# Strassen's seven half products for eight in the attention scores of the first two chunks

## The chip, the cores and the metric

The kernel runs on one core of a Trainium2 chip. The metric is the device time of one execution in microseconds. A core has five engines with a queue each: TensorE (PE, with its weight loads shown as PEld), VectorE (DVE), ScalarE (ACT), GpSimd (POOL) and SyncE (SP), and 16 DMA engines that move data between HBM and the on-chip memory. [...]

## The reference

A graph of N = 2708 nodes with 512 features goes through four layers, each followed by a residual and a layer norm. Layer 2 is two attention layers in a row, and the change is in these alone:

```
proj = x @ W                      # W: 512 x 1024
Wh, Ws = jnp.split(proj, 2, axis=-1)
scores = Wh @ Ws.T                # 2708 x 2708, contraction over 512
a = softmax(scores, axis=-1) * adj
out = a @ Wh + x
x = leaky_relu(out, 0.01)
```

adj is a sparse 0/1 matrix of about 16 neighbours a node, so a has few entries that count. Everything is float32.

## The kernel before

Nodes are cut in 22 blocks of 128 rows (the last has 20), and the columns of a product in six chunks `CH` of 512, 512, 512, 512, 384 and 276 nodes. Both weight halves of an attention layer are multiplied into one 512x512 matrix (`mix`), so that scores are x M x^T. `project_steps` (L1491) computes for each chunk k four tiles `wst[k][c]`, c being the quarter of the contraction, of 128 x 512, and the rows `z` = Wh, which go to a table `pairs` in HBM.

`layer` (L1827) then walks over the six chunks. For chunk k, `load_moving` (L1542) brings the four tiles `xs` (128 x chunk) that stream through PE. `scores` (L1552) computes the scores of one block of 128 nodes against the whole chunk: four matmuls (c = 0..3) of weights 128x128 into one PSUM bank, which ACT copies to a page `s`. The order of blocks is 0, 1, 2, 21, 3 to 20. Block 21 with its 20 rows takes one pass of four small matmuls side by side (`few`, L673) and four adds by DVE. `greatest` (L1578) keeps a running maximum `top` over the blocks. In the next chunk's walk `shift_rows` (L1586) transposes `top` after block 1, reduces and broadcasts it (`wide`), and `shift_columns` transposes `wide` back after block 2 and copies it to `shift`.

From block 3 on, `soften` (L1623) works on the chunk before, one or two steps after each block: DVE subtracts `shift`, ACT takes Exp, DVE adds to the sum and multiplies by the mask (one byte a node, `load_masks` brings all six groups at once), and SP stores the block to `pairs`. When a chunk is softened, `fetch` (L1677) lets POOL gather by an index list the few rows of `pairs` that a block of nodes needs, with at most ten gathers ahead, and `weigh` (L1732) multiplies them on PE into `acc`, between the score products of later chunks. `end` (L1768) divides, adds the residual and stores. After the last chunk the rest is softened and weighed between the work of a filler: the projection of the second attention layer, or the first products of layer 3.

The order of the instructions on every engine is written out: class `Ordered` (L54) chains each engine's instructions in the order in which the program issues them. Where in the walk a gather is weighed is decided by a clock that counts the ideal time of products (`advance`, with `cost(columns)` = 4 x columns / 2400 us) and takes a gather to need 1.15 us and to land 6 us later. No measured time enters. Tiles of on-chip memory come from a pool of 82 pages of 2 KB a partition, PSUM from two halves of four banks (`bank`): score products take half 0, and `acc`, transposes and the like take half 1. A page or bank that is used again makes the first writer wait for its last readers.

All engine work is recorded at one helper line, L71, in the profile; groups are told apart by their tiles: sp for score products, acc for the sparse products of the outer layers and for the weighing (acc<-g), z and wst for projection, mm for the dense products.

Of the kernel before, what the change touches and what calls it, by code (L numbers as in the profile page):

```python
# [19 lines left out]
P = 128  # L20
# [22 lines left out]
PAGES, WIDES = 82, 11  # L43
# [44 lines left out]
class Kernel:  # L88


    def __init__(self, ctx, tc, x_in, x_t, adj, adj_t, w0, b0, w1, b1, w2, w2_t, w3, b3, out):
        self.tc, self.nc = tc, tc.nc
        nc = self.nc
        self.ctx = ctx
        self.x_in, self.x_t, self.adj, self.adj_t, self.out = x_in, x_t, adj, adj_t, out
        self.w0, self.b0, self.w1, self.b1, self.w2 = w0, b0, w1, b1, w2
        self.w2_t, self.w3, self.b3 = w2_t, w3, b3
        const = ctx.enter_context(tc.tile_pool(name="const", bufs=1))
        self.small = ctx.enter_context(tc.tile_pool(name="small", bufs=4))
        scratch = ctx.enter_context(tc.tile_pool(name="scratch", bufs=1, space=DRAM))  # L100
        tile_ = lambda name, shape, dt: const.tile(shape, dt, tag=name, name=name)
        self.ident = tile_("ident", [P, P], FP)
        self.ones = tile_("ones", [P, P], FP)
        self.ones_b = tile_("ones_b", [P, P], BF)

        self.rdeg = tile_("rdeg", [P, NB], FP)
        self.dis = tile_("dis", [P, NB], FP)
        self.nbad = len(CH) * NB
        self.bad = tile_("bad", [P, self.nbad + NB], FP)


        self.feeds = tile_("feeds", [P, NB, QUARTERS, NB], BF)
        self.givers = tile_("givers", [P, NB, LISTS], I32)

        self.base = tile_("base", [P, QUARTERS], FP)
        self.upto = tile_("upto", [P, P], BF)
        self.node = tile_("node", [P, 1], FP)
        self.block = tile_("block", [P, NB], BF)
        self.since = tile_("since", [P, P], BF)
        self.saved = [  # L120
            [scratch.tile([P, D], FP, tag=f"x{s}_{i}", name=f"x{s}_{i}") for i in range(NB)]
            for s in range(3)
        ]
        self.between = [
            scratch.tile([P, D], FP, tag=f"y_{i}", name=f"y_{i}") for i in range(NB)
        ]

        self.masks = [
            scratch.tile([P, NB, w], U8, tag=f"mask{k}", name=f"mask{k}")
            for k, (_, w) in enumerate(CH)  # L130
        ]

        self.turned = [
            [
                scratch.tile([P, DC, w], FP, tag=f"t{s}_{k}", name=f"t{s}_{k}")
                for k, (_, w) in enumerate(CH)
            ]
            for s in range(2)
        ]

    def constants(self, page):
# [4 lines left out]
        nc.gpsimd.memset(self.feeds, 0.0)  # L146
# [313 lines left out]
    def other_weights(self):  # L460


        nc = self.nc
        with self.tc.tile_pool(name="ps_bad", bufs=1, space=PSUM) as ps_bad:
            total = self.small.tile([P, 1], FP, tag="bad_sum", name="bad_sum")
            nc.vector.tensor_reduce(total, self.bad, AX.X, ALU.add)
            ps = ps_bad.tile([P, 1], FP, tag="bad", name="bad_ps")
            nc.tensor.matmul(ps, self.ones, total, start=True, stop=True)
            flag = self.small.tile([P, 1], I32, tag="flag", name="flag")
            nc.vector.tensor_scalar_min(flag, ps, 1.0)  # L470
        return nc.values_load(flag[0:1, 0:1])


def blocks_of(k):

    c0, cw = CH[k]
    return [(c0 // P + q, q * P, min(P, cw - q * P)) for q in range(-(-cw // P))]

# [37 lines left out]
class Fast:  # L516
# [4 lines left out]
    def __init__(self, kernel):  # L521
        self.k, self.tc = kernel, kernel.tc
        self.nc = Ordered(kernel.tc)
        self.notes = []
# [10 lines left out]
    def run(self):  # L535
        kernel, nc = self.k, self.nc
        with ExitStack() as ctx:
# [4 lines left out]
            self.small, self.lists = pool("small_f", 4), pool("lists", 1)  # L542
# [295 lines left out]
    def note(self, k, g, at):  # L838

        (c0, cw), (j0, j1) = CH[k], GROUPS[g]  # L840
        feeds = self.k.feeds.rearrange("p i q j -> p j (i q)")
        i0, full = c0 // QW, cw // QW
        sets = [(j0, j1, P)] if j1 < NB else [(j0, j1 - 1, P), (j1 - 1, j1, QW)]
        for q0, q1, n in ((0, full, QW), (full, -(-cw // QW), cw % QW)):
            for a, b, rows in sets if q0 < q1 else ():
                v = at[:rows, a - j0 : b - j0, q0 * QW : q0 * QW + (q1 - q0) * n]
                self.nc.vector.tensor_reduce(
                    feeds[:rows, a:b, i0 + q0 : i0 + q1],
# [351 lines left out]
    def index(self, k):  # L1200
# [8 lines left out]
        tile_ = lambda tag, shape, dt: self.lists.tile(shape, dt, tag=tag, name=f"{tag}{k}")  # L1209
# [31 lines left out]
        f = kernel.feeds[:, i0 : i0 + n, :, :]  # L1241
        nc.vector.tensor_scalar(f, f, 0.0, None, ALU.not_equal)
        some, a, b = (tile_(t, one, BF) for t in ("some", "a", "b"))
# [13 lines left out]
        kept = tile_("kept", one, BF)  # L1257
# [26 lines left out]
        def examine():  # L1284

            top = tile_("top", [P, n], FP)
# [13 lines left out]
        row, which = tile_("row", one, BF), tile_("which", one, BF)  # L1300
# [5 lines left out]
        sums = tile_("sums", [P, n, 2 * LISTS], FP)  # L1306
# [16 lines left out]
        t = tile_("list", [P, n, LISTS], FP)  # L1323
# [5 lines left out]
    def one_hot(self, s, row, which):  # L1329
# [12 lines left out]
        tile_ = lambda tag, w: self.lists.tile([P, NB, w], BF, tag=tag, name=f"{tag}{s}", bufs=2)  # L1342
        hit, both = tile_("hit", LISTS), tile_("both", 2 * LISTS)
# [13 lines left out]
class Chunk:  # L1357


    def __init__(self, ly, k):  # L1360
# [3 lines left out]
        self.s, self.masks, self.ends = {}, {}, []  # L1364
        self.softened = 0
        self.fetched, self.rden = [], None
# [12 lines left out]
class AttentionLayer:  # L1379
    def __init__(self, number, pairs):  # L1380
        self.number, self.pairs = number, pairs
        self.w, self.mixed, self.xt, self.wst = [], [], {}, {}


class Attention:
# [7 lines left out]
    def __init__(self, fast):  # L1393
# [16 lines left out]
        self.mixed = self.scratch.tile([DC, P, D], FP, tag="mixed", name="mixed")  # L1410
        self.layers = [AttentionLayer(a, self.pairs[a]) for a in range(2)]
        self.clock, self.fetch_free, self.pending = 0.0, 0.0, []

# [77 lines left out]
    def project_steps(self, ly, k):  # L1491
# [4 lines left out]
        for m in range(DC):  # L1496
# [13 lines left out]
            yield True  # L1510
        for i, lo, n in blocks_of(k):
# [29 lines left out]

    def load_moving(self, ch):  # L1542
# [9 lines left out]
    def scores(self, ch, j):  # L1552
# [6 lines left out]
        if n <= QW:  # L1559
            ps = self.f.few(  # L1560
                0, name, n, cw, lambda c: wst[c][:, lo : lo + n], lambda c: ch.xt[c][:, :cw]
            )
            self.f.total(s[:n, :cw], ps, n, cw)
            self.advance(cost(cw))
# [10 lines left out]
        nc.scalar.copy(s[:n, :cw], ps[:n, :cw])  # L1575
        self.advance(DC * cost(cw))

    def greatest(self, ch, j):  # L1578
        n, cw, s = rows_of(j), ch.cw, ch.s[j]
        if j == 1:  # L1580
            ch.top = self.page(f"top{ch.name}")
            self.nc.vector.tensor_max(ch.top[:, :cw], ch.s[0][:, :cw], s[:, :cw])
        elif j > 1:
            self.nc.vector.tensor_max(ch.top[:n, :cw], ch.top[:n, :cw], s[:n, :cw])
# [31 lines left out]
    def load_masks(self, ch):  # L1616
        for j0, j1 in GROUPS:
            a = self.page(f"a{ch.name}_{j0}", U8, (P, DC, ch.cw))
            self.nc.sync.dma_start(a[:, : j1 - j0, :], self.k.masks[ch.k][:, j0:j1, :])
            for j in range(j0, j1):  # L1620
                ch.masks[j] = a[:, j - j0, :]

    def soften(self, ch):  # L1623
# [4 lines left out]
        if v < NB:  # L1628
            if v == 0 and ch.k >= 2:

                assert not self.chunks[ch.k - 2].to_fetch
            n = rows_of(v)
            s = ch.s[v][:n, :cw]
            nc.vector.tensor_sub(s, s, ch.shift[:n, :cw])
            nc.scalar.activation(s, s, AF.Exp)
        j = v - 1
        if j < 0:
            return
        n = rows_of(j)
# [37 lines left out]
    def fetch(self, ch):  # L1677
# [19 lines left out]
        begin = max(self.fetch_free, self.clock + (16 if (q, t) == ch.first_fetch else 0))  # L1697
# [3 lines left out]
    def load_rows(self, ch, q):  # L1701
# [7 lines left out]
        if ch.ly.number == 1:  # L1709
            ch.first[q] = self.page(f"x1{ch.name}_{q}")  # L1710
            self.nc.sync.dma_start(ch.first[q][:w], self.k.saved[1][i][:w])

    def fetch_ahead(self):
        count = sum(len(c.fetched) for c in self.chunks)
        for c in self.chunks:
            while c.to_fetch:
                if c.softened <= NB or count >= self.AHEAD:
                    return
# [13 lines left out]
    def weigh(self, wait=False):  # L1732
# [16 lines left out]
        if first:  # L1749
            ch.acc = self.bank(1, f"acc{ch.name}_{q}")  # L1750
        for h, g in enumerate(gs):
# [74 lines left out]

    def layer(self, ly, chunks, fill):  # L1827
        f = self.f
        self.chunks, self.made = chunks, {}
        for k, ch in enumerate(chunks):  # L1830
            old = chunks[k - 1] if k else None


            js = [0, 1, 2, NB - 1, *range(3, NB - 1)]
            for n, j in enumerate(js):
                if old and n == 0:
                    self.load_masks(old)
                if old and n >= 3:
                    if n == 3 and k >= 3:
                        while chunks[k - 3].to_weigh:  # L1840
                            self.weigh(True)
                    for _ in range(1 + n % 2):
                        if old.softened <= NB:
                            self.soften(old)
                self.scores(ch, j)
# [3 lines left out]
                if n == 4 and k + 1 < len(chunks):  # L1849
                    self.load_moving(chunks[k + 1])  # L1850
                if k + 1 == len(chunks) and n in ((5, 11, 19) if ly.number == 0 else (5, 11)):
                    next(fill)
                if old and n == 0:
                    self.greatest(old, js[-1])
                if n:
                    self.greatest(ch, js[n - 1])
# [4 lines left out]
                if old and n == 1:  # L1861
                    self.shift_rows(old)
                if old and n == 2:
                    self.shift_columns(old)
        last = chunks[-1]
        self.load_masks(last)
        self.greatest(last, js[-1])
# [7 lines left out]

        done = self.clock + (2 if ly.number == 0 else 4)
        while last.softened <= NB:
# [108 lines left out]
```

## Time and profile before

| what | value |
|---|---|
| device time, median of 3 runs | 2330.78 us (2322.93 to 2333.93) |
| span of the profiled execution, first to last instruction | 2297.7 us |
| PE busy | 2269.4 us, 99% of the span |
| DVE, ACT, POOL busy | 1391.5, 675.5, 705.4 us |
| TensorE clock granted, mean | 0.997 |
| score products sp, records of 512, 384 and 276 columns | 1344, 336 and 336 |
| score products sp, busy (a record's overlap with the next counted once) | 589.9, 114.9 and 83.4 us |
| gathers | 510 |

No device time is given for the profiled execution itself; its span is 33.1 us below the median of the runs. Busy time is the union of an engine's records. A float32 matmul leaves two records. A record's own length holds the run through the array, so the pace of back-to-back matmuls is read from the distance of their starts, or from the length of a stretch over its count. In the chain of work that ended last, each piece is what released the next. The lines that the prediction rests on are shown there.

### The profile page before, as it was taken

To read this page: it belongs to the slowest core of one execution; us is meant where nothing else is said; L and a number is where in the kernel's file an instruction comes from. 1 tells how busy PE (TensorE), PEld (TensorE's weight loads), DVE (VectorE), ACT (ScalarE), POOL (GpSimd) and SP (SyncE) were. 2 spreads that over 40 slices of the span, in tenths; PEclk is the share of its full clock that TensorE was granted. 3 is DMA by queue.
4 is the path that set the end of the run, shared out by engine and by line. 5 is a ranking of instruction groups with operands and counts; after the bars stand their busy time and mean duration, and the time that the engine had idled before them with its cause. 6 is when DMAs were issued, how large, how long until landed. Compare 5 with 4: busy or idle time off the path is not lost.

```text
span 2297.7 us, 25903 instructions
## 1 busy us (share of the span) xinstructions
PE 2269.4 (99%) x8525; PEld 1289.0 (56%) x8525; DVE 1391.5 (61%) x2803; ACT 675.5 (29%) x1354; POOL 705.4 (31%) x822
## 2 busy tenths in 40 slices
PE   9999999999999999999999999999999999899997
PEld 6776876777644444443555444444443555466685
DVE  6777787786553537748667511238769788525523
ACT  7444452322111123223322200113223334342211
POOL 3433431111000001635557540001635467442000
PEclk9999999999999999999999999999999999999999
DMA  9966752223547415858789997405868799963311
GB/s 351 286 188 184 199 168 81 76 81 104 208 184 267 144 25 184 303 191 297 254 311 360 349 412 284 183 8 179 303 218 286 254 322 339 334 217 120 116 51 43
DMA packets 260929, 486.34 MB, mean 212 GB/s; under 512 B 40238, under 2 KB 126950, under 8 KB 260784
## 3 DMA queue, kind: packets, MB, share of 16 engines
q1 hardware_dynamic: 192128, 269.63, 33.6%
q0 software_dynamic: 68656, 214.96, 28.0%
q8 instruction: 69, 1.13, 0.2%
q14 instruction: 76, 0.62, 0.1%
HBM read 307.55 MB, written 176.92 MB: 211 GB/s over the span
## 4 chain that ended last, share of the span: by engine, by line
PE 86%; DMA 6%; DVE 4%; ACT 1%; issue 1%; POOL 1%; SPq 0%; ACTq 0%; POOLq 0%; DVEq 0%
PE sp L71 33%; PE acc L71 30%; PE mm L71 8%; PE z L71 6%; PE wst L71 6%; DMA x<-x 2%; DMA x<-in_x 1%; DMA at<-in_adj_t 1%; DMA g<-pairs,givers 1%; PE mix L71 1%; DMA pairs<-s 1%; POOL xt L71 1%; PE list L71 1%; ACT m L71 1%; PE tr_x2t L71 0%
## 5 line engine op out<-in xcount | busy, mean ns | idle before, releaser
L71 PE MATMUL sp<-xs,wst_sb 128*128 128x512 f32 (+3 forms) x2112 | 798.3, 544 | 0.0
L71 POOL DMA_INDIRECT g<-pairs,givers x510 | 524.2, 1028 | 872.9 <-issue 338.9
L71 PEld LDWEIGHTS sp<-xs,wst_sb 128*128 128x128 f32 (+1 forms) x2112 | 379.7, 186 | 408.4 <-issue 324.8
L71 PE MATMUL acc<-m,xh 128*128 128x512 f32 (+4 forms) x1584 | 566.8, 379 | 6.6 <-ACT m L71 5.1
L71 PE MATMUL acc<-m,xl 128*128 128x512 f32 (+4 forms) x1584 | 549.6, 365 | 2.0 <-DVE xl L71 1.8
L71 PEld LDWEIGHTS acc<-m,xh 128*128 128x128 f32 (+1 forms) x1584 | 288.0, 188 | 70.9 <-issue 21.3
L71 PEld LDWEIGHTS acc<-m,xl 128*128 128x128 f32 (+1 forms) x1584 | 288.3, 188 | 46.3 <-issue 5.3
L71 PE MATMUL acc<-g 128*32 128x512 f32 (+1 forms) x1020 | 264.8, 606 | 4.6 <-DMA g<-pairs,givers 4.0
L71 ACT COPY s<-sp 128x512 f32<-128x512 f32 (+2 forms) x252 | 132.7, 528 | 396.8 <-PE sp L71 395.1
L71 ACT ACTIVATE s<-s 128x512 f32<-128x512 f32 (+3 forms) x264 | 151.6, 580 | 319.8 <-DVE s L71 319.5
L71 DVE TENSOR_TENSOR top<-top,s 128x512 f32<-128x512 f32 (+2 forms) x240 | 149.1, 621 | 156.1 <-ACT s L71 154.5
L71 PE MATMUL mm<-w,ht 128*128 128x512 f32 (+1 forms) x528 | 223.7, 593 | 0.0
L71 ACT CAST m<-at 128x512 fp32r<-128x512 uint8 (+5 forms) x396 | 199.2, 567 | 62.3 <-DMA at<-mask 19.7
L71 DVE TENSOR_TENSOR s<-s,shift 128x512 f32<-128x512 f32 (+3 forms) x264 | 162.7, 620 | 36.2 <-ACT shift L71 36.2
L71 DVE TENSOR_TENSOR s<-s,a 128x512 f32<-128x512 f32 (+3 forms) x264 | 165.8, 628 | 13.6 <-DMA a<-mask 4.5
L71 DVE TENSOR_TENSOR sum<-sum,s 128x512 f32<-128x512 f32 (+4 forms) x252 | 156.5, 621 | 15.4 <-ACT s L71 15.4
L71 PEld LDWEIGHTS mm<-w,ht 128*128 128x128 f32 (+1 forms) x528 | 95.8, 186 | 117.0 <-issue 112.2
L71 PEld LDWEIGHTS acc<-g 128*32 128x32 f32 (+1 forms) x1020 | 74.6, 134 | 148.0 <-issue 116.5
L71 PE MATMUL z<-w,xt 128*128 128x512 f32 (+1 forms) x352 | 151.0, 596 | 0.0
L71 PE MATMUL wst<-xt,mixed 128*128 128x512 f32 (+2 forms) x384 | 150.5, 544 | 0.0
L71 POOL DMA_DIRECT2D x<-o x44 | 26.0, 597 | 329.7 <-DVE o L71 325.4
L71 PEld LDWEIGHTS wst<-xt,mixed 128*128 128x128 f32 x384 | 72.0, 190 | 71.1 <-issue 58.8
(168 smaller groups left out, 1476.7 us busy)
## 6 DMA issues: line engine op xcount, KB each, us to landing
pairs<-z_sb SPq DMA_DIRECT2D x84, 768.0 KB
pairs<-s SPq DMA_DIRECT2D x168, 256.0 KB
at<-in_adj_t SPq DMA_DIRECT2D x84, 256.0 KB
xres<-x POOLq DMA_DIRECT2D x44, 256.0 KB, 4.6
x<-o POOLq DMA_DIRECT2D x43, 256.0 KB, 3.4
pairs<-s SPq DMA_DIRECT2D x84, 128.0 KB
x<-x SPq DMA_DIRECT2D x37, 256.0 KB
at<-mask SPq DMA_DIRECT2D x32, 256.0 KB
```

The source lines that it names most:

```text
L71: ins = call(*args, **kw)
```

## The change

In chunks 0 and 1 of each attention layer (`SEVEN`) the scores of two blocks of 128 nodes are computed together. The contraction of 512 is cut in two halves, the two blocks are the two rows, and the chunk of 512 is cut in two halves of 256 columns. Eight half products (2 x 2 x 2) become seven, by the scheme of Strassen in Winograd's form, with sums of operands before and sums of results after. Blocks 0 to 17, 19 and 20 form ten pairs (for chunks 0 to 3 of the weights blocks b and b+2; for chunks 4 and 5 blocks b and b+1). Block 18 and block 21 are done as before.

Operand sums: `sum_weights` makes S1 = A21+A22, S2 = S1-A11 and S4 = A12-S2 during projection and saves the quarter A21 to HBM; `replace` overwrites A21 by S3 = A11-A21 when first needed; `restore` loads A21 back in chunk 1 and at the start of chunk 2. For weight chunks 0 to 3 the sums are three pages each, stored in chunk 0 (`keep_sums`) and loaded again in chunk 1 (`load_sums`). `sum_moving` and `replace_moving` do the same for the chunk's own tiles.

Besides, the walk is rearranged for all chunks: Exp and the sum follow the subtraction by one step each (two in chunks 0 and 1); softening may go on into the walk after the next; the maxima are taken one step later, so that `shift_rows` comes after block 2 and `shift_columns` after block 21; masks are loaded group by group, two ahead (five from chunk 4 on); the tiles of the next chunk are loaded at step 15 for 4; `x1` rows are loaded at the first weighing of a block for at its first gather. The pool has 87 pages for 82. The feeds of the index lists, and the lists' work tiles, move from pools of their own to pages. The check for unusual weights multiplies by a bf16 matrix of ones.

```diff
-PAGES, WIDES = 82, 11
+PAGES, WIDES = 87, 11
+STREAMED = 4
+FIRST_LANDS = 16
+SOFT = NB + 2 * 2
+ALONE = 18
+SEVEN = [0, 1]
...
+        if k not in self.feeds:
+            self.feeds[k] = self.page(f"feeds{k}", BF, (P, len(blocks_of(k)), QUARTERS, NB))
+            self.nc.gpsimd.memset(self.feeds[k], 0.0)
...
+    def sum_weights(self, ly, k):
...
+        for c in range(2):
+            nc.vector.tensor_add(tiles["s1"][c], a21[c], a22[c])
+            nc.vector.tensor_sub(tiles["s2"][c], tiles["s1"][c], a11[c])
+            nc.vector.tensor_sub(tiles["s4"][c], a12[c], tiles["s2"][c])
+            nc.sync.dma_start(self.quarter[ly.number][k][c], a21[c])
...
+    PRODUCTS = {
+        1: ("a11", "b11"),
+        2: ("a12", "b21"),
+        3: ("s4", "b22"),
+        4: ("a22", "t4"),
+        5: ("s1", "t1"),
+        6: ("s2", "t2"),
+        7: ("s3", "t3"),
+    }
...
+        def ahead(t):
+            self.product(ch, t, 2, t["y"][:, :h], start=True)
+            self.product(ch, t, 5, t["y"][:, h:cw], start=True)
+            nc.scalar.copy(t["r"][:, h:cw], t["y"][:, h:cw])
+
+        def one(t):
+            t["x"] = self.bank(t["n"] % 3 // 2, f"spx{t['name']}")[:, :h]
+            self.product(ch, t, 1, t["x"], start=True)
+            nc.scalar.copy(t["s"][:, :h], t["x"])
+
+        def six(t):
+            self.product(ch, t, 3, t["y"][:, h:cw])
+            self.product(ch, t, 6, t["x"])
+            nc.scalar.copy(t["s"][:, h:cw], t["x"])
+
+        def seven(t):
+            self.product(ch, t, 7, t["x"])
+            t["v"] = self.page(f"v{t['name']}")
+            nc.scalar.copy(t["v"][:, :h], t["x"])
+
+        def four(t):
+            self.product(ch, t, 4, t["x"])
+            nc.scalar.copy(t["r"][:, :h], t["x"])
+            ch.complete.append(t["j"][1])
+
+        def first_block(t):
+            nc.vector.tensor_add(t["s"][:, :cw], t["s"][:, :cw], t["y"][:, :cw])
+            ch.complete.append(t["j"][0])
+
+        def second_block(t):
+            nc.vector.tensor_add(t["r"][:, h:cw], t["r"][:, h:cw], t["v"][:, :h])
+
+        older = old = None
+        for n, p in enumerate(pairs):
+            self.replace(ch.ly, p[0])
+            if ch.k == 0 and p[0] in groups and p[1] == 0:
+                self.keep_sums(ch.ly, p[0])
+            t = begin(n, p)
+            ahead(t)
+            if old:
+                first_block(old)
+            yield "mid"
+            one(t)
+            if older:
+                four(older)
+            if ch.k and p[1] == 0 and p[0] + 1 in groups:
+                self.load_sums(ch.ly, p[0] + 1)
+            if following and p == pairs[-2]:
+                self.load_sums(ch.ly, 0)
+            yield "end"
+            if old:
+                seven(old)
+            yield "mid"
+            six(t)
+            if old:
+                second_block(old)
+            older, old = old, t
+            yield "end"
...
+        j = v - ch.apart
+        if 0 <= j < NB:
+            s = ch.s[j][: rows_of(j), :cw]
             nc.scalar.activation(s, s, AF.Exp)
-        j = v - 1
+        j -= ch.apart
...
+        if j == 0 and ch.k >= 2:
+            while self.chunks[ch.k - 2].to_fetch:
+                self.weigh(True)
...
+            for what in self.walk(ch):
+                if what == "mid":
+                    self.soften_next()
+                    self.weigh()
+                    continue
+                n += 1
+                if old and n < old.masks_ahead:
+                    self.load_mask(old, n)
...
+                if old and n < 2:
+                    self.greatest(old, last=n == 1)
+                many = 2 if len(self.to_soften) > 1 else 1 + n % 2
+                for _ in range(0 if ch.seven else many):
+                    self.soften_next()
...
-                if old and n == 1:
-                    self.shift_rows(old)
                 if old and n == 2:
+                    self.shift_rows(old)
+                if old and n == 3:
                     self.shift_columns(old)
+                    self.to_soften.append(old)
```

## The prediction

> **What bounds the kernel now.** I read the shares of busy time first, then the chain that ended last, then windows of 50 us. The header, the first two parts and the chain:
>
> ```profile
> span 2297.7 us, 25903 instructions
> PE 2269.4 (99%) x8525; PEld 1289.0 (56%) x8525; DVE 1391.5 (61%) x2803; ACT 675.5 (29%) x1354; POOL 705.4 (31%) x822
> PE 86%; DMA 6%; DVE 4%; ACT 1%; issue 1%; POOL 1%; SPq 0%; ACTq 0%; POOLq 0%; DVEq 0%
> PE sp L71 33%; PE acc L71 30%; PE mm L71 8%; PE z L71 6%; PE wst L71 6%; DMA x<-x 2%; DMA x<-in_x 1%; DMA at<-in_adj_t 1%; DMA g<-pairs,givers 1%; PE mix L71 1%; DMA pairs<-s 1%; POOL xt L71 1%; PE list L71 1%; ACT m L71 1%; PE tr_x2t L71 0%
> ```
>
> TensorE (PE) is busy almost throughout, and the score products (sp) are a third of the chain. So work taken from sp comes off the end, unless something else then makes PE wait. The windows say how near that is (columns: stretch, its length, then busy us of PE, weight load, DVE, ACT, POOL, then clock, DMA share, GB/s):
>
> ```profile
> 850.00:900.00 50.00, 50.00 (x118) 22.14 (x117) 49.20 (x80) 19.58 (x35) 0.00 (x0) 1.00 0.40 127
> 900.00:950.00 50.00, 50.00 (x150) 21.06 (x148) 30.50 (x49) 11.98 (x21) 29.98 (x30) 1.00 0.79 267
> 1950.00:2000.00 50.00, 42.66 (x150) 22.29 (x148) 26.23 (x62) 17.75 (x33) 26.96 (x30) 0.95 0.94 351
> ```
>
> 850 to 900 is the second chunk of attention layer 0, one of those that change: PE is full, but VectorE (DVE) is at 98% too. 1950 to 2000 is the tail of layer 1, the one stretch of attention where PE waits. The rates of back-to-back work come from the chain in order of time (start, us, what, count) and from DVE's timeline:
>
> ```profile
> 854.79 61.37 PE sp L71 x143
> 1225.31 3.72 PE sp L71 x16
> 576.45 4.01 PE acc L71 x32
> 859.75 0.68 DVE L71 TENSOR_TENSOR top<-top,s 128x512 f32<-128x512 f32 x1
> 860.35 0.68 DVE L71 TENSOR_TENSOR s<-s,shift 128x512 f32<-128x512 f32 x1
> 860.95 0.69 DVE L71 TENSOR_TENSOR sum<-sum,s 128x512 f32<-128x512 f32 x1
> 861.67 0.69 DVE L71 TENSOR_TENSOR s<-s,a 128x512 f32<-128x512 f32 x1
> 862.28 0.68 DVE L71 TENSOR_TENSOR top<-top,s 128x512 f32<-128x512 f32 x1
> ```
>
> A float32 product leaves two records. One of 512 columns takes 61.37/143 = 0.429 us, one of 276 columns (last chunk) 3.72/16 = 0.2325. The line through both gives 0.2158 us at 256 columns. The acc row is fp32r with 276 columns: 4.01/32 = 0.125 us for each with its own 128x128 weight load, so a load can hide under 0.125 us. DVE's starts are 0.60, 0.60, 0.72 and 0.61 us apart, though each record lasts 0.68.
>
> **What the Trainium skill says.** "TensorE: Matmul & The Clock Gate", section "Back-to-back issue gap", gives N/2.4 + 2.5 ns for a warm pass, and "FP8 and Floating Point Precision", section "TensorE Precision Notes", four passes for true FP32: an estimate of 4 x 215.8 = 863 ns for a product of 512 columns; the trace has 2 x 429 = 858. At 256 columns it gives 437, or 218 per record, beside my 215.8. The first page's section "LDWEIGHTS (loading the stationary operand)" puts a 128-column load at P/1.2 = 107 ns; the trace, with one every 125 ns, allows that. "VectorE: DVE Perf Modes", section on the TRN2 errata, gives (N+151)/0.96 ns for a float32 tensor_tensor: 691 at 512 columns, and the trace has 686; in a row they start closer.
>
> **The change part by part.**
>
> *PE.* In four chunks (k = 0, 1 of two layers) 20 of 22 blocks go in 10 pairs. A pair had 8 products of 512 columns, 16 records x 0.429 = 6.87 us; now 7 x 2 products of 256 columns, 28 records x 0.2158 = 6.04. That is 0.82 us for each of 40 pairs, -33 us. Bounds: at 0.2145 (half of 0.429) -34; at the 276-column 0.2325, -14. Block 18 and the 20-row block stay.
>
> *ACT.* A pair has five 256-column copies for two of 512. Rows of 580 ns at 512 and 375 at 276 give 358 at 256: 1.8 us beside 1.2. With two Exp of 0.63 that is 3.1 us in a PE pair of 6.0: hidden. The third product of a pair writes where the fifth was copied out, the sixth where the first was; two or three other products (1.7 to 2.6 us) lie between, against 0.36 us for a copy, and Exp now follows its subtraction by two steps. I take 0; were ACT held by DVE, PE would wait as long.
>
> *DVE.* In the second chunk a pair now has two softening steps of 0.60 + 0.72 + 0.61 = 1.93, two maxima of 0.61, one 512-column sum from PSUM (three such adds in a row of the 20-row block took 2.12, so 0.71) and one 256-column sum (276 columns take 0.37 to 0.40 a start in the tail; 0.38): 3.86 + 1.21 + 0.71 + 0.38 = 6.16 us, against PE's 6.04. DVE falls behind by 0.12 us a pair over 8 pairs, 1 us. The four banks of half 0 forgive it: a pair's y bank is needed again only when PE has gone on about 4 us. In the first chunk of each layer DVE has 11.6 us of work in 50. The operand sums cost 6 adds per weight chunk (36 x 0.38 = 14 us a layer) during projection, where DVE is at 18 to 27 in 50, and 6 per moving chunk. The first of the latter (2.3 us) stands before product 5 but behind the lone block's 3.43 us: 0 to 1 us. I take +1 a layer for lag and +0.5 for this.
>
> *Chunk ends.* Maxima are gathered one step later, so the row transpose follows block 2 and the column transpose follows the 20-row block. Before, a whole block (3.43 us) lay between the two; now 1.05 us, while the reduce (0.72), the broadcast copy (0.4) and two hand-overs need about 1.3. In the third chunk no weighing fills the gap, and DVE still has softening steps in front: 0.3 us plus the lag, I take 1.5 (bounds 0 and 5). Later chunks have gathers to weigh: 0.2 each. That makes +2 a layer.
>
> *DMA.* Each layer stores 12 pages of operand sums in its first chunk (3.1 MB, where the DMA share is near 0) and loads them back in the second, in groups of three, with about 9.4 us of PE work ahead of use (the first group 13). Quarters of the weights, 1.3 MB, go out and come back. A 256 KB page lands in 4.6 us (xres) to 6.3 (x on POOL); DMA is at 40% there, so three pages fit: 0. SP, which issues them, stands behind pair stores that wait for DVE; behind the loads stand masks asked for two groups ahead. If cover went, each us late would be a us of PE, four groups a layer.
>
> *Gathers.* The first chunk has 17 softening steps in the second chunk and ends at block 5 of the third, not in the second, so its gathers start 9 blocks of PE work later. Its 48 gathers took 70 us (903.8 to 973.8); a chunk with weighing takes 100 us, and POOL was free for 22 us before the next (995.6). The next is softened at the end of the third chunk, so they fit: 0. Later chunks are softened one or two blocks later. In layer 1's tail PE idles 11 us between 1900 and 2050 already; one more softening step of 1.4 us, against masks loaded earlier and the x1 rows loaded at the first weighing: I take +1, bounds -8 and +12.
>
> *Projection, pages, early layers.* Fourteen more pages live through projection, five more exist, and feeds and lists now come from them: 0, hidden by round-robin reuse; a missed store would show as ACT waiting. The feeds memsets are six short POOL instructions.
>
> Sum: -33 + 2 x (1.5 + 2) + 1 = -25 us. Span 2297.7 becomes 2273. The profiled execution's time lies in what is around the span: the median of the three runs is 2330.8, 33 us above the span (launch and end, not in it), so I add the same 33: 2306 us.
>
> **Rivals.** (a) *VectorE bounds the second chunk*: if a pair costs it 7.3 us (six half-width ops at their full record length), PE waits 1.3 us x 8 pairs x 2 = 20: 2326. For it: 49.2 of 50 busy. Against: starts 0.60 apart. (b) *Half width is not half time*: at 0.2325 or more the gain is 14 or less: 2325; at 0.245 none, 2339. Against: a record every 0.125 us in acc. This is also the case that the change does not do what it says. (c) *Slower: the reloads of operand sums are late.* Place: products 5, 3 and 6 of the second chunk. Price: landing minus 9.4 us, eight groups. In the tail x<-x took 12 us under a full DMA; at 14 us it is 8 x 4.6 = 37: 2343. It decides from 12.6 us on; at 40% DMA share I doubt it. (d) *The tail moves* by its bounds: 2297 to 2317.
>
> **How the numbers follow.** Chances: my forecast 0.58, (a) 0.13, (b) 0.09, (c) 0.08, (d) 0.12. No change is within 0.5%, 11.7 us, 2319.1 to 2342.4. Faster: all of the forecast, all of (d), a few hundredths of (a) and (b): 0.76. Same: most of (a) and (b), a part of (c): 0.18. Slower: 0.06. The range 2290 to 2328 holds the forecast, (d) and (a), and leaves out (c) and the worse half of (b). The forecast's own range is 2297 to 2315.
>
> **What would show it.** Right: spx and spy records of 256 columns about 0.215 us apart; the changed chunks 8 us shorter each (the second 66 for 74); PE at 50.00 in 50 in them. Wrong: PE waiting for DVE at spy (a); records at 0.23 and more (b); PE waiting for DMA s1, s2 or s4 (c); PE idling over 20 us between the end of layer 1's scores and the next 100 us (d); or PE waiting for wide at the column transpose by several us in each chunk.

## The result and the profile after

| | kernel before | changed kernel |
|---|---|---|
| device time, median of 8 runs each | 2325.34 us (2314.42 to 2333.93) | 2298.77 us (2294.11 to 2313.41) |
| ratio, with its 95% interval | | 0.9895 (0.9869 to 0.9921) |
| a second measurement on another chip, medians | 2303.64 us | 2280.09 us |
| its ratio | | 0.9910 (0.9896 to 0.9925) |

The change makes the kernel faster by 0.9 to 1.05%, 21 to 24 us by the ratios. I had forecast 24.8 us (2330.8 to 2306). The medians of the kernel before on the three chips of the runs below are 2320.0, 2303.6 and 2304.6 us, 0.7% apart, so what follows compares ratios to the kernel before, each measured on the same chip.

The header, the busy times and the chain that ended last, of the changed kernel:

```profile
span 2292.7 us, 27402 instructions
PE 2247.8 (98%) x9004; PEld 1383.1 (60%) x9004; DVE 1477.7 (64%) x3012; ACT 691.1 (30%) x1474; POOL 714.4 (31%) x827
PE 77%; DVE 8%; DMA 7%; issue 3%; ACT 2%; SPq 1%; POOL 1%; another core or an unknown queue 0%; DVEq 0%; ACTq 0%; POOLq 0%
PE acc L71 28%; PE sp L71 18%; PE mm L71 8%; PE spx L71 6%; PE z L71 5%; PE wst L71 5%; PE spy L71 4%; DVE s L71 2%; DMA pairs<-s 1%; DMA at<-in_adj_t 1%; DMA g<-pairs,givers 1%; DVE sum L71 1%; SPq L71 1%; DMA xt<-t 1%; DMA x<-in_x 1%
```

Score products fell from 33% of the chain to 28% (sp, spx and spy), but DVE, DMA and issue now hold 18% of it, where they had 11%. PE is busy for 21.6 us less, and idle for 44.9 us where it was for 28.3. The profile before is that of a quick execution, though: in a second profile of the kernel before (span 2316.7) PE is idle for 40.8 us, and in a second one of the changed kernel (span 2278.7) for 36.7. The chain in order of time (start, us, what, count) gives the pace of the half-width products; then two windows in the columns of the prediction, of the second chunk and of the tail:

```profile
792.79 1.73 PE spy L71 x8
794.52 2.59 PE spx L71 x12
```

```profile
850.00:900.00 50.00, 50.00 (x225) 42.51 (x224) 45.91 (x77) 23.65 (x56) 0.00 (x0) 1.00 0.48 150
1950.00:2000.00 50.00, 43.85 (x143) 21.33 (x142) 29.14 (x68) 15.99 (x33) 32.61 (x32) 1.00 0.93 321
```

2.59/12 = 0.2158 us a record, to the digit what was forecast. The second chunk keeps PE at 50.00 of 50, with DVE at 45.9. Its length is read from its first whole block of scores to that of the third chunk, in PE's timeline of the second profile:

```profile
833.30 3.60 PE L71 MATMUL sp<-xs,wst_sb 128*128 128x512 f32 x8
899.25 3.60 PE L71 MATMUL sp<-xs,wst_sb 128*128 128x512 f32 x8
```

That is 66.0 us, where I had said 66. Where PE waits instead (waited for, us in total, times, longest), and two windows of 10 us around the two longest waits:

```profile
PE acc L71 <- issue: 7.2, 5, 5.8
PE tr_mx L71 <- DVE wide L71: 5.0, 4, 3.6
...
PE spx L71 <- DVE s L71: 1.7, 1, 1.7
```

```profile
1110.00:1120.00 10.00, 8.39 (x20) 5.12 (x21) 5.96 (x11) 2.03 (x4) 0.00 (x0) 0.66 0.43 141
1930.00:1940.00 10.00, 4.21 (x10) 3.01 (x10) 9.53 (x19) 7.20 (x14) 7.22 (x7) 0.66 1.04 382
```

The 3.6 us wait is the column transpose at the end of layer 0's fourth chunk. The 5.8 us wait is at the first low-part product (acc<-m,xl) of the closing layer. The view puts it down to "issue", but the timelines show that VectorE had not made the operand xl: it begins to at 1935.69, and PE goes on at 1936.42:

```profile
1935.69 4.95 DVE L71 SCALAR_TENSOR_TENSOR xl<-x,xh 128x512 fp32r<-128x512 f32 x8
1936.42 0.80 PE L71 MATMUL acc<-m,xl 128*128 128x512 f32 x1 [5.79 <-issue]
```

In both windows of 10 us the granted clock is 0.66.

### The profile page after: what moved, and what is told of

Same layout as the page of the kernel before. It is cut to its first block, busy times and chain, and to the rows that moved or that the text cites. A ratio compares the mean times of both kernels' runs of the same rounds, so it can differ in the third digit from the quotient of the medians.

```text
span 2292.7 us, 27402 instructions
## 1 busy us (share of the span) xinstructions
PE 2247.8 (98%) x9004; PEld 1383.1 (60%) x9004; DVE 1477.7 (64%) x3012; ACT 691.1 (30%) x1474; POOL 714.4 (31%) x827
## 4 chain that ended last, share of the span: by engine, by line
PE 77%; DVE 8%; DMA 7%; issue 3%; ACT 2%; SPq 1%; POOL 1%; another core or an unknown queue 0%; DVEq 0%; ACTq 0%; POOLq 0%
PE acc L71 28%; PE sp L71 18%; PE mm L71 8%; PE spx L71 6%; PE z L71 5%; PE wst L71 5%; PE spy L71 4%; DVE s L71 2%; DMA pairs<-s 1%; DMA at<-in_adj_t 1%; DMA g<-pairs,givers 1%; DVE sum L71 1%; SPq L71 1%; DMA xt<-t 1%; DMA x<-in_x 1%
## 5 line engine op out<-in xcount | busy, mean ns | idle before, releaser
L71 POOL DMA_INDIRECT g<-pairs,givers x510 | 532.8, 1045 | 867.8 <-issue 373.5
L71 PE MATMUL sp<-xs,wst_sb 128*128 128x512 f32 (+5 forms) x1472 | 523.7, 525 | 0.0
L71 PEld LDWEIGHTS sp<-xs,wst_sb 128*128 128x128 f32 (+1 forms) x1472 | 260.7, 185 | 249.7 <-issue 186.2
L71 PE MATMUL acc<-g 128*32 128x512 f32 (+1 forms) x1020 | 270.4, 606 | 6.8 <-DMA g<-pairs,givers 4.7
L71 ACT COPY s<-sp 128x512 f32<-128x512 f32 (+2 forms) x172 | 87.4, 509 | 439.4 <-PE sp L71 249.2
L71 ACT CAST m<-at 128x512 fp32r<-128x512 uint8 (+5 forms) x396 | 198.9, 567 | 43.9 <-DMA at<-mask 27.1
L71 DVE TENSOR_TENSOR top<-top,s 128x512 f32<-128x512 f32 (+3 forms) x240 | 149.3, 622 | 20.0 <-ACT s L71 11.9
```

Of the source, the lines that this page charges most:

```text
L71: ins = call(*args, **kw)
```

## Experiments

Ratios are to the kernel before on the same chip; 0.001 is 2.3 us.

**The kernel before again.**

> The kernel before itself, run once more, with the span of each of its runs. My forecast took 33 us to lie around the span, the profiled 2297.7 us against the 2330.8 us of the clock. The rival reading, which the runs of the changed kernel suggest (time less span is 1.8 us in each): the spans of the kernel before lie between 2312 and 2332 us, its times 1.8 us above them, and the execution profiled before was an unusually quick one. First reading: spans near 2298 us under times of 2315 to 2334 us.

Ratio 0.9998 (0.9982 to 1.0014). In its 14 runs the time lies 1.9 to 2.05 us above the span, and the spans go from 2309 to 2327 us. So 2 us lie around a span, not 33. Whether the 2297.7 us came from a quicker chip or a quick execution cannot be told: on two other chips the kernel before has medians of 2303.6 and 2304.6 us.

**An eighth product.** The seventh product is computed and added twice, so the output is not the reference's.

```diff
             self.product(ch, t, 7, t["x"])
+            self.product(ch, t, 7, t["x"])
```

> The changed kernel with the seventh product of each pair computed and added twice, so that its output is not the reference's: four more records of 256 columns a pair, 40 pairs x 4 x 0.2158 = 34.5 us of TensorE work and nothing else. Theory 1 (TensorE sets the pace in both chunks): 34 us above the changed kernel, ratio to the kernel before about 1.0045. Rival (VectorE sets the pace in the second chunk, so TensorE has slack there): about 17 us above the changed kernel, ratio about 0.997.

Ratio 1.0058 (1.0033 to 1.0084), so 34 to 38 us above the changed kernel (0.9910 and 0.9895). Starts of tr_top at the first two chunk ends of layer 0, in PE's timelines of the changed kernel (its second profile) and of this one:

```profile
843.10 0.60 PE L71 MATMUL tr_top<-ident,top 128*128 128x128 f32 x4
910.42 0.60 PE L71 MATMUL tr_top<-ident,top 128*128 128x128 f32 x4
```

```profile
854.42 0.60 PE L71 MATMUL tr_top<-ident,top 128*128 128x128 f32 x4
930.38 0.60 PE L71 MATMUL tr_top<-ident,top 128*128 128x128 f32 x4
```

From one to the other it takes 67.3 us, and 76.0 us with the eighth product: 8.6 us more, and 10 pairs x 4 x 0.2158 are 8.6. (The 67.3 is more than the chunk's 66.0 because tr_top comes 9.8 us behind the start of the second chunk, but 11.2 us behind that of the third.) Added PE work is paid in full there; VectorE does not set the pace.

**The parts of the machinery.** The rearrangement alone (no chunk in seven products, no sums of weights); the same with the sums of weights formed and the quarter A21 stored and read back (the sums themselves are neither stored nor loaded again, which happens only in chunks of seven products); the first chunk alone; the second chunk alone:

```diff
-SEVEN = [0, 1]
+SEVEN = []            # walk; sums keeps the next line
-        self.sum_weights(ly, k)
```

```diff
-SEVEN = [0, 1]
+SEVEN = [0]           # first
```

```diff
-SEVEN = [0, 1]
+SEVEN = [1]           # second
-            if ch.k == 0 and p[0] in groups and p[1] == 0:
+            if ch.k == 1 and p[0] in groups and p[1] == 0:
...
-            if ch.k and p[1] == 0 and p[0] + 1 in groups:
+            if ch.k > 1 and p[1] == 0 and p[0] + 1 in groups:
...
-                if not ch.seven and n == 1:
+                if not ch.seven and n == 1 and ch.k > 1:
```

> The changed kernel with no chunk in seven products and without the sums of the weights: only its other order of work, its 87 pages and its rearranged lists are left, and every chunk takes its sixteen records of 512 columns a pair of blocks. Theory 1 (my forecast: all of the gain is TensorE's work, the rearrangement costs 0 to 3 us): the time of the kernel before, ratio 0.998 to 1.002. Theory 2 (part of the gain is the new order of the work): ratio 0.996 or below. Theory 3 (the new order costs what the profile after lost between the third chunk's start and the second layer's scores, 8 to 13 us): ratio 1.0035 to 1.0055.

> No chunk in seven products, as in the run with the rearrangement alone, but the sums of the weights are formed during the projection, a quarter of the weights is stored and read back at the first chunk: the fixed part of the machinery, which does not depend on how many chunks use it. The runs so far fit one price: 16.5 us saved for each of the two chunks, and some 6 to 8 us of fixed cost on top of the rearrangement's 5.6 us (the first chunk alone gave 8.4 us over the rearrangement, the second alone 9.7 us, both 26 to 30 us). If that fixed cost is here: ratio 1.005 to 1.006, some 12 us over the kernel before. If the sums are hidden, as I forecast (nothing for the sums, the stores and the reloads): ratio 1.0025 as with the rearrangement alone, and what is missing in the single chunks lies in their own stores, reloads and moving operands.

> Seven products in the first chunk of each layer alone, so half of the TensorE work saved, 16.5 us of 32.9 us. Theory 1: half the gain of the changed kernel, ratio about 0.9945 (12 to 14 us under the kernel before). Rival (in the second chunk VectorE, with 6.16 us a pair against TensorE's 6.04 us, eats the gain): nearly the whole gain is already here, ratio 0.991 or below. Rival the other way (the arrangement costs 8 to 13 us whatever number of chunks uses it): ratio 0.997 to 1.000.

> Seven products in the second chunk of each layer alone; the sums of the weights wait in their pages through the first chunk, are stored during the second, and the operands are put back after it. If the two chunks add up, the seven products being worth 30 us over the arrangement alone (from 5.6 us above the kernel before to 24 us below it) and the first chunk having given 8.4 us of that: 21 us here, ratio about 0.993. If each chunk saves its 15 us and the run with the first chunk alone lost 7 us to waits of its own: 9 us under the kernel before, ratio about 0.996. If VectorE sets the pace in the second chunk: next to nothing over the arrangement alone, ratio 1.000 or above.

| seven products in | ratio | 95% interval |
|---|---|---|
| none (walk) | 1.0025 | 1.0010 to 1.0040 |
| none, sums formed (sums) | 1.0035 | 1.0022 to 1.0048 |
| first chunk (first) | 0.9988 | 0.9973 to 1.0004 |
| second chunk (second) | 0.9981 | 0.9971 to 0.9992 |
| both (the change) | 0.9895, 0.9910 | 0.9869 to 0.9921, 0.9896 to 0.9925 |

The rearrangement costs 6 us, with the sums 8 us (the intervals of the two overlap, so the sums may be free). The twelve that one theory gave the two together are not there. From sums to the change it is 29 to 32 us, and in the profiles PE is busy for 31.2 us less (2273.3 and 2242.0); TensorE's saved work is 32.9. The waits of PE from 1100 us on without any seven products, of the run with the sums:

```profile
PE acc L71 <- DVE xl L71: 7.0, 2, 6.3
PE tr_mx L71 <- DVE wide L71: 3.8, 7, 0.7
```

So the long wait at the closing layer's xl (6.3 us at once, where the two profiles of the kernel before have 1.8 and 1.1) comes with the rearrangement, not with Strassen's scheme. So do the small waits at tr_mx, of 0.3 to 0.7 us at nearly every chunk end; but long ones there do not belong to it alone, since the second profile of the kernel before has one of 2.8 us. Each chunk alone gives less than half: 1.0035 less 16.5 us (0.0071) would be 0.9964, and 4 to 6 us are missing, though by the intervals it can be near nothing. Their profiles show waits with slow clock (first: 2.6 and 3.1 us at tr_mx; second: 7.0 us at xl), but why these two variants meet more of them than the change does is not settled.

**The two waits taken away.** Two gathered groups multiplied ahead of the closing layer's products, and tr_mx a block later:

```diff
         self.greatest(last, last=True)
+        if ly.number == 1:
+            self.weigh(True)
+            self.weigh(True)
```

```diff
-                if old and n == 3:
+                if old and n == 4:
                     self.shift_columns(old)
```

> The changed kernel, with two gathered groups of the second layer multiplied between its last block of scores and the first products of the closing layer, so that TensorE has work while VectorE finishes the softening of the fifth chunk and then the low parts (xl). If the wait of 5.8 us there (7.6 and 8.3 us in the runs with the rearrangement alone and with the eighth product, 1.8 us before) and the slow clock behind it are a loss of the rearrangement: 4 to 9 us under the changed kernel, ratio to the kernel before about 0.987. If the gathered rows have not landed by then, or the end is set elsewhere: within 2 us of the changed kernel, a wait on a gather standing in place of the wait on xl.

> The changed kernel, with the transposes of the widened maxima (tr_mx) of each chunk one block of scores later, so that a whole block more lies between them and the transposes before (tr_top). My chunk-end term: PE's waits at tr_mx, 7.4 us in all, go but for about 1 us of the 3.6 us one, with the slow clock behind that: 5 to 9 us under the changed kernel. Rival: VectorE and the softening, which start a block later, hand the time back at the end of the layers: within 2 us of the changed kernel, or slower by up to 5 us.

Ratios 0.9897 (0.9882 to 0.9912) and 0.9908 (0.9895 to 0.9922), beside 0.9910 for the changed kernel on the same chip:

> The changed kernel itself, as the mark for the runs beside it. From its first measurement: ratio 0.9895 (0.987 to 0.992), some 24 us under the kernel before. If all of TensorE's 32.9 us and the 5.6 us by which the rearrangement alone was slower are added: 27 us under it, ratio 0.988.

The first run is 3 us better, which the intervals don't separate from nothing. Its waits from 1900 us on, and then those of the second:

```profile
PE acc L71 <- DMA g<-pairs,givers: 3.9, 11, 1.0
PE acc L71 <- DVE xl L71: 0.5, 2, 0.2
```

```profile
PE acc L71 <- DVE xl L71: 5.9, 2, 5.3
PE acc L71 <- ACT m L71: 3.6, 2, 2.0
```

With the gathered groups in front, PE no longer waits long for xl; but the second profile of the changed kernel has no long wait there either (0.7 us), so the wait comes in some executions only, and the mean gain is small. With tr_mx a block later no wait for wide is left at all, where the second profile of the changed kernel had 4.2 us of them (8 waits, at most 0.7), and the time is the same. As I read it, softening starts a block later, VectorE comes late to xl, and the 5.3 us wait there hands the time back. This is not shown, since waits of that length stand there in other runs too.

**Longer waits at the chunk ends.**

```diff
-            nc.vector.tensor_copy(
-                ch.wide[:n, q0:q1, :],
-                mx[:n, q0:q1].unsqueeze(2).to_broadcast([n, q1 - q0, P]),
-            )
+            for _ in range(9 if ch.k < len(CH) - 1 else 1):
+                nc.vector.tensor_copy(
+                    ch.wide[:n, q0:q1, :],
+                    mx[:n, q0:q1].unsqueeze(2).to_broadcast([n, q1 - q0, P]),
+                )
```

> The changed kernel, with VectorE copying the widened maxima nine times in place of once at the ends of the first five chunks of each layer: 8 x 0.36 us more ahead of tr_mx at eight ends, 8 x 0.28 us at two, 27 us of PE waiting in all, none of it covered, since PE waits there already. If a PE wait costs its own length: 27 us over the changed kernel, ratio about 1.002. If the granted clock falls behind each wait of some 3.5 us, as after the waits of 3.6 us and 5.8 us in the profile of the changed kernel (0.66 over ten us, so 3.4 us more each): 45 to 60 us, ratio 1.010 to 1.017, and dips of the clock at the ten places in the profile.

Ratio 1.0158 (1.0131 to 1.0185): 57 to 61 us above the changed kernel. Busy times of the changed kernel's second profile (span 2278.7), of this one (span 2337.5), and of this one the waits and two windows:

```profile
PE 2242.0 (98%) x9004; PEld 1382.6 (61%) x9004; DVE 1477.9 (65%) x3012; ACT 691.0 (30%) x1474; POOL 718.0 (32%) x827
```

```profile
PE 2261.3 (97%) x9004; PEld 1395.1 (60%) x9004; DVE 1515.6 (65%) x3092; ACT 690.8 (30%) x1474; POOL 713.3 (31%) x827
```

```profile
PE tr_mx L71 <- DVE wide L71: 43.9, 10, 5.4
```

```profile
850.00:860.00 10.00, 6.82 (x27) 5.95 (x28) 7.55 (x15) 1.74 (x5) 0.00 (x0) 0.83 0.00 0
920.00:930.00 10.00, 5.95 (x20) 2.88 (x13) 9.52 (x19) 1.93 (x4) 0.00 (x0) 0.83 0.11 37
```

The copies took longer than I had put them, so PE waits 43.9 us where it was 4.2: 39.7 more. The same 9004 records are busy for 19.3 us longer. The two make 59.0 of the span's 58.8. Not all of it comes from the copies: 3.4 us have arisen before the first of them, in the early layers (the first wait of spx ends at 782.4 us for 779.0), which leaves 55.4. The clock dips behind nine of the ten waits (3.5 to 5.4 us each); behind the one of 3.5 us at 1564 us it does not.

**VectorE's room, and a third chunk.** A pass of 128 x 512 more a pair in the second chunk; and the third chunk in seven products too, together with the two gathered groups from above:

```diff
             nc.vector.tensor_add(t["s"][:, :cw], t["s"][:, :cw], t["y"][:, :cw])
+            if ch.k:
+                nc.vector.tensor_max(t["s"][:, :cw], t["s"][:, :cw], t["s"][:, :cw])
```

```diff
-SEVEN = [0, 1]
+SEVEN = [0, 1, 2]
```

> The changed kernel with one more VectorE pass over 128 x 512 a pair in the second chunk of each layer (the larger of a block and itself): 20 x 0.69 us = 13.8 us of VectorE work. If VectorE stands at the edge there, as my 6.16 us against 6.04 us a pair had it: 14 to 16 us over the changed kernel, ratio about 0.997. By the windows of the profile after (45.9 and 48.0 us busy of 50, so 0.25 to 0.5 us a pair to spare): 4 to 9 us, ratio 0.992 to 0.994. If VectorE has room after all: nothing, ratio 0.990.

> The changed kernel with the two gathered groups ahead of the closing layer's products (ratio 0.9897 so far), and the third chunk of each layer in seven products as well: 20 pairs more, 16.5 us of TensorE work less. If only TensorE counts: ratio about 0.983. Rival: in the third chunk VectorE has the softening of the second and the gathered rows of the first chunk beside the sums of the products, about 6.2 us a pair plus 3.6 us a gathered block, and sets the pace, with more pages held: no gain or a loss, ratio 0.989 or above.

The added pass: ratio 0.9935 (0.9913 to 0.9957), 6 to 9 us above the changed kernel. The second chunk itself is no longer (849.47 to 916.78 us between the two tr_top, 67.3 again). VectorE's lag is paid at its end, first in the changed kernel's second profile, then here:

```profile
912.35 0.66 PE L71 MATMUL tr_mx<-ident,wide 128*128 128x128 f32 x4 [0.35 <-DVE wide L71]
```

```profile
922.44 0.66 PE L71 MATMUL tr_mx<-ident,wide 128*128 128x128 f32 x4 [4.08 <-DVE wide L71]
```

Ten passes at the 0.60 us between starts that the prediction read add 6.0 us, and 3.7 us of them come out. By this estimate VectorE had 2.3 us of room in the chunk, 0.2 us a pair.

The third chunk: ratio 0.9874 (0.9849 to 0.9898), the lowest here, but 5 us under the run with the gathered groups alone (0.9897), not 16, and the intervals of the two overlap. Its layer 0 is 14 us shorter than in that run from the first scores to mix (463.0 us for 476.9). Then projection takes 4 us more and layer 1 takes 7 us more (642.9 for 636.3): 13 of POOL's instructions, which issue the gathers, fewer fall into layer 0 and 13 more into the projection, and PE waits 9.7 us for wide, for 4.2. So part of the gathered products is put off, not gone.

## Why the prediction was right

Lengths of stages, from the PE timelines of the kernel before (two profiles), of the rearrangement alone and of the change (second profile), in us:

| stage | before | before, again | walk | change |
|---|---|---|---|---|
| early layers | 760.2 | 768.1 | 763.1 | 765.4 |
| layer 0, first scores to mix | 493.0 | 501.0 | 495.5 | 477.5 |
| mix to layer 1's first scores | 203.0 | 203.7 | 208.8 | 209.1 |
| layer 1, first scores to the closing layer's mm | 654.5 | 657.0 | 661.0 | 639.6 |
| rest | 187.0 | 186.9 | 187.6 | 187.1 |
| span | 2297.7 | 2316.7 | 2316.0 | 2278.7 |

The two profiles of one kernel differ by 8 us in a stage, so differences of a few us between single profiles prove nothing; the gain and the cost given below rest on the ratios.

*PE, -33 us:* right. The record is 0.2158 us, the second chunk takes 66.0 us for 74.2 (I had said 66 for 74), and eight against seven products in one arrangement make 34 to 38 us (eight), the change against sums 29 to 32. Rival (b), half width is not half time, is out.

*DVE, +1 a layer and +0.5 for the first sum:* the lag was over-sized, since 6.16 us a pair is above what VectorE needs: by the dve run it has about 0.2 us a pair to spare under PE's 6.04. Rival (a) is out, but the room is small, and the dve run shows where the lag would appear: at the chunk's end. Product 5 of the first pair does not wait for its sum. What waits, in layer 0 alone, is a later spx, for 1.7 us, until VectorE has done the adds of the 20-row block (second profile):

```profile
770.54 3.22 DVE L71 TENSOR_TENSOR at_row<-upto,plan 128x1024 bf16<-128x1024 bf16 x3
776.86 2.12 DVE L71 TENSOR_TENSOR s<-s,sp 20x512 f32<-20x512 f32 x3
779.03 2.00 PE L71 MATMUL spx<-xs,wst_sb 128*128 128x256 f32 x8 [1.68 <-DVE s L71]
```

In front of these adds stand about 4 us of work on the index lists (at_row, marks), which layer 1 does not have there. This was in none of my terms.

*Chunk ends, +2 a layer:* the size was right where the run is quiet (4.2 us in all), the place was not. I had the third chunk take most of it; each later end of a layer's chunks has 0.35 to 0.74 us, the first none. In the first profile after, one wait of 3.6 us stands at the fourth. Just before it ACT's copies of the turned rows (x2b) and VectorE's reduce were released by something that the profile names only as remote. In walk, first and eight the same place has 2.7 to 3.4 us, in the second profile of the change 0.7. What it waits for there is not settled.

*Tail of layer 1, +1 (-8 to +12):* within the bounds, but probably too small. The wait on xl was 5.3 to 8.3 us in seven of the twelve profiles of the rearranged kernels (after, walk, second, eight, sums, cols, and first, where 6.1 us at the same place are put down to ACT's m), and 1.8 and 1.1 us before. In the changed kernel's first profile PE gets to the closing layer's products while VectorE still has softening steps and four maxima in front of xl. The slow clock around it, 3.4 to 5.2 us lost by the windows of 10 us, was in none of my terms.

*Reloads of operand sums, 0:* right; no profile has PE waiting for s1, s2 or s4 (the run with the sums has one wait of 0.6 us for a quarter read back). Rival (c) is out. *Projection, 0:* sums against walk is +2 us, within the intervals; the 5 to 6 us more between mix and layer 1 in the table come with 12 more PE records in walk (617 for 605), and 12 are missing before mix (1576 for 1588), so I take most of it for moved work.

*33 us around the span:* this step failed. It is 2 us. The profiled execution was simply quicker than those behind the median. The forecast of 2306 us came out near because the difference of two spans may be carried to a median whatever lies around a span; the reason given for it was wrong.

In sum: -33 for TensorE and +8 for the rest was the forecast. Measured are -29 to -38 for TensorE, and +6 to +8 for the rearrangement with its sums. The mechanism was right: PE's saved work comes off the end, less a few us that the new order costs. That the +8 agrees in size is partly luck. A share of it, 3 us, was for VectorE's lag and sums in chunks of seven products, and walk and sums, which have no such chunk, lose the 6 to 8 us without it. VectorE's lateness at xl and at wide, and clock lost behind these waits, are what their profiles show; but taking away the waits at wide gained nothing, and those at xl 3 us within the noise, so what the 6 to 8 us are made of stays open.

## What to carry to other kernels

Here one engine was busy 99% of the span, and work taken from it came off the end nearly in full, 29 to 32 us of 32.9, even with its neighbour busy for 92% of the stretch. The neighbour's lag, when it was made to appear, showed at the next hand-over that had no other work in front, so look there. Ask what follows a wait, too: ten added waits of TensorE cost 1.4 to 1.5 times their own length (55.4 us of span, or 57 to 61 by the ratios, for 39.7 us of waiting). And when an arrangement and a saving come in one change, run the arrangement alone: here it cost 6 to 8 us, and whether a better order at the tail wins some of it back is not shown.

## What the runs showed of the hardware

Many waits of PE here are followed by slow products. Behind the 5.8 us wait the products of the closing layer start 0.43 us apart until 1940.0 us, and then 0.23. The Trainium skill has the mechanism in "TensorE: Matmul & The Clock Gate", section "What's actually happening": an idle window of about 3.4 us drops the clock to half, and a busy one of about the same length brings it back. I had priced every wait at its own length. The trace agrees on the price: the dips lose 1.7 us (0.83 over 10 us), 3.4 us (0.66, or 0.83 twice), at the tail also 5.2 us (second: 0.50 and 0.98), and once 6.8 us (dve, 90 to 120 us: 0.87, 0.50 and 0.95), one to four times half of 3.4. It differs on when, and gives no threshold. Waits of 2.6 us (first, at 1030 us) and 2.7 us (walk, at 1125) were followed by 0.84 and 0.83, and so were two waits of only 0.7 us each, 1.2 us apart, in the second profile of the change. But the 1.7 us at spx was not, nor was one of the ten waits of the late run, 3.5 us long. The two short waits and the window that holds their dip:

```profile
1979.68 0.50 PE L71 MATMUL acc<-m,xh 128*128 128x512 f32 x1 [0.71 <-ACT m L71]
1980.89 0.50 PE L71 MATMUL acc<-m,xl 128*128 128x512 f32 x1 [0.72 <-DVE xl L71]
```

```profile
1980.00:1990.00 10.00, 9.28 (x32) 6.73 (x32) 9.56 (x23) 7.46 (x17) 3.74 (x6) 0.83 0.81 252
```

This also goes with the spread of the runs. Over the 49 runs of the kernel before on one chip, a straight line through time and mean granted clock has 3.0 us for each 0.001 (correlation -0.74); the clock alone would make 2.3. The rest may be the waits themselves, which is not shown. One that varies stands in the early layers (acc<-m,xh at 96 to 101 us): it is 1.6 to 6.4 us long in every profile but the first of the kernel before, and 3.8 us in the second of that kernel, so it is not the change that brings it.
